# Attention scores and values as 64x64 products on TensorE, with the upper values split in two

## Chip, cores and metric

The kernel runs on one core of one Trainium2 chip. The metric is the device time of one execution in microseconds (us); the time before is the median of three executions. An additional execution was taken by the hardware profiler, and all lines of a profile below come from that one execution.

A core has five engines that run side by side and wait for one another through semaphores: TensorE (PE in the profile; PEld is its loading of weights), VectorE (DVE), ScalarE (ACT), GpSimd (POOL), and SyncE (SP), which here only issues DMAs. Each engine works through its own instructions in the order of the program. A matmul takes a stationary operand (weights) and streams the columns of a moving operand past it, into a bank of PSUM. The array of 128x128 cells can be used in tiles of 128x64, 64x128 or 64x64 cells; products at different places of the array run at the same time.

## What is computed

64 sequences of 128 tokens and 512 features go through one layer of multi-query attention: 16 query heads of 64 features share one key head and one value head, with a bias per head, a learned null key and value in front, a causal mask and a key mask. The result is projected, normalized and added to the input.

```python
xn = layernorm(x, g_in)                                # x: [64, 128, 512]
q = (xn @ Wq).reshape(b, n, H, DH).transpose(0, 2, 1, 3) * scale   # H = 16, DH = 64
k, v = split(xn @ Wkv)                                 # one head of 64 each
k, v = concat(null_k, k), concat(null_v, v)
sim = einsum('bhid,bjd->bhij', q, k) + concat(null_bias, attn_bias)
sim = where(causal, sim, neg); sim = where(mask, sim, neg)
out = einsum('bhij,bjd->bhid', softmax(sim), v)
out = out.transpose(0, 2, 1, 3).reshape(b, n, H * DH) @ Wo
return x + layernorm(out, g_out)
```

Everything is float32.

## The kernel before

The order of all instructions is written out by hand: `step(n)` (L838) is called for n from -6 to 62, and each call issues pieces of several stages for different sequences: normalizing (n+10, n+12), queries of a group of four sequences (`qg`), keys and values (n+5, n+6), scores (n+2), softmax (n+1), values (n), output projection (n-1 and earlier). There is no scheduler, so the order in the source is the order on each engine.

**Scores.** The 16 heads fall into two groups u of 8, and within a group a head is told by the row half r (which half of the array's rows its 64 features lie in) and by f (0 to 3). Partitions 0 to 63 of the score tile `S[b]` hold group u=0, partitions 64 to 127 group u=1, for 64 queries each. `scores(b, 0)` (L476) makes the lower scores: queries 0 to 63, which see keys 0 to 63 alone, as 16 products of 64x64 weights and 64 columns. `scores(b, 1)` makes the upper scores: queries 64 to 127 with all 128 keys. Before the change it does so as 8 products whose weights are 64 rows by 128 columns (both groups side by side). The row half r also chooses the PSUM bank: `pv[:, r]`. There is a single score buffer (pool `ps_s`, one buffer, tag "s"), so the upper (second) scores wait until DVE's `scores_add(b, 0)` (L509) has taken the lower (first) ones out. DVE then forms row maxima (`scores_max`), ACT the exponentials (L525), POOL multiplies with the reciprocal sums (L546).

**Turning the weights round.** `blocks_T(b)` (L569) turns S[b] on DVE in blocks of 32x32 into the tile `sb` (one buffer), and `blocks_move(b)` (L578) issues 14 DMAs on the SP queue that carry the blocks to the partitions where they belong, into `aTb` (one buffer except at the end). `aTb[keys, slot, head, query]` has six slots of 32 queries: slots 0 and 1 for the lower queries (group u=0 on partitions 0 to 63, u=1 on 64 to 127), slots 2 and 3 for the upper queries of u=0, slots 4 and 5 for those of u=1, with 128 keys each. The DMAs take eight semaphores in turn, so each also waits until the DMA eight places before it has landed.

**Values.** `values(b)` (L631) uses two PSUM tiles of pool `ps_w` (tag "w", two buffers), `po_b_0` and `po_b_1`, one for each group u, a bank each. `half` 0 holds the lower queries: 4 products with 64 key rows, the lower rows (`lo`) into bank 0, the upper rows (`hi`, with values moved up in `nv`) into bank 1. `half` 1 holds the upper queries: 4 products with all 128 key rows and 64 output partitions. Each product has 256 columns. ACT then moves both banks to `oT[b]` (L655). The two `ps_w` buffers are next used by `pk` (keys and values of a later sequence, L1017) and by a query product (`pw`).

**Around them in a step.** The queries and the output projection are made with seven products in place of eight (`product` L405, `out_product` L702), the sums and differences for which POOL forms: `token_sum` (L391), `out_sums` (L692). Pairs of sequences are projected together: a step with even n has `third` (a pair is normalized and added to the input on DVE: `pair_norm`, `pair_residual` L765), a step with odd n has `second` (`out_sums` and most of a pair's products). So steps come in kinds:

| n mod 4 | what differs near the end of the step |
|---|---|
| 0, 2 (even) | `pair_residual(p4 + 1)` runs on DVE (L767, L768) ahead of `blocks_T(n + 1)` |
| 1 | just before, `tokens_in` has issued four DMAs `xT<-xd` (L294) on SP, then `nulls_move` two; `mask_neg` runs on DVE once per group |
| 3 | nothing of these |

The stretch in question is the end of `step` (L981 to L1011):

```python
        if ok(n + 2):
            scores(n + 2, 0)
            scores_add(n + 2, 0)
        ...
        if third:
            pair_residual(p4 + 1)
        if soft and n + 1 < B - 2:
            blocks_T(n + 1)
        if ok(n + 2):
            scores_max(n + 2, 0)
        ...
        if ok(n):
            values(n)
        ...
        if n + 1 in sbs:
            blocks_move(n + 1)
        if ok(n + 2):
            scores(n + 2, 1)
```

`blocks_T(n + 1)` overwrites `sb`, so it waits for the DMAs of `blocks_move(n)`; `blocks_move(n + 1)` overwrites `aTb`, so it waits for the value products of n. POOL's `bias_add(n + 3)` reuses the score tile and waits for `blocks_T(n + 1)`. After the stretch PE goes on with a query product `pa` (k = 6), `pk`, `pa` (k = 7), and, over the next step's start, products into `pa` and `pc`; `pc` is freed by DVE's L442 (`q_out` into `qT`), which needs ACT's copy `ku` (L432) too.

Of the kernel before, what the change touches and what calls it, by code (L numbers as in the profile page):

```python
# [17 lines left out]
def kernel(  # L18
# [11 lines left out]
    g_out: bass.AP,  # L30
    out: bass.AP,
):

# [442 lines left out]
    def scores(b, hf):  # L476
        g, t = divmod(b, GB)
        nk = N if hf == 1 else NL
        ps = ps_s.tile([P, 2, NF, N], FP, tag="s", name=f"ps_{b}_{hf}")
        pv = ps.rearrange("p r f j -> p r (f j)")[:, :, 0 : NF * nk].rearrange(  # L480
            "p r (f j) -> p r f j", f=NF
        )
        for f in range(NF):
            if hf == 1:
                for r in range(2):
                    rows = slice(r * DH, (r + 1) * DH)
                    nc.tensor.matmul(  # L487
                        pv[:, r, f, :],
                        qT[g][rows, f, t, 1].rearrange("p u i -> p (u i)"),
                        kT[b][rows, :],  # L490
                        start=True,
                        stop=True,
                    )
            else:
                for r in range(2):
                    rows = slice(r * DH, (r + 1) * DH)
                    for u in range(2):
                        nc.tensor.matmul(  # L498
                            pv[u * DH : (u + 1) * DH, r, f, :],
                            qT[g][rows, f, t, 0, u],  # L500
                            kT[b][rows, 0:NL],
                            start=True,
                            stop=True,
                        )
        pss[b, hf] = pv

    pss = {}
# [120 lines left out]
            pt.rearrange("p e (s q) -> p e s q", q=Q),  # L628
        )

    def values(b):  # L631
        g, t = divmod(b, GB)
        oT[b] = bp.tile([P, NC, N], FP, tag="oT", name=f"oT_{b}")
        po = [
            ps_w.tile([P, 2, 2, NF, Q], FP, tag="w", name=f"po_{b}_{u}")
            for u in range(2)
        ]
        lo, hi = slice(0, DH), slice(DH, P)
        parts = [
            (0, 0, lo, vs[g][lo, t, 0:DH], slice(0, 2)),  # L640
            (1, 0, hi, nv[g][hi, t, 0:DH], slice(0, 2)),
            (0, 1, slice(0, P), vs[g][:, t, 0:DH], slice(2, 4)),
            (1, 1, slice(0, P), vs[g][:, t, 0:DH], slice(4, 6)),
        ]
        for u, half, rows, vals, slots in parts:
            for r in range(2):
                nc.tensor.matmul(  # L647
                    po[u][r * DH : (r + 1) * DH, half],
                    vals,
                    aT_of(b)[rows, slots, r * NF : (r + 1) * NF],  # L650
                    start=True,
                    stop=True,
                )
# [184 lines left out]
    def step(n):  # L838
# [145 lines left out]
            if ok(n + 1) and fill:  # L984
                rinv(n + 1, 1)
                scale(n + 1, 1)
        if third:
            pair_residual(p4 + 1)
        if soft and n + 1 < B - 2:
# [2 lines left out]
            scores_max(n + 2, 0)  # L992
        if n == 0:
            blocks_T(1)
        if n == B - 2:
            attn_T_pe(n)
        if ok(n):
            values(n)
        elif fast:
            product(qg, f, 6, ps_q, "a", start=False)  # L1000
            keep("a", "u2")
        if n + 1 in sbs:
            blocks_move(n + 1)
# [96 lines left out]

    load_res(B - 1)
    attn_T_pe(B - 1)
    values(B - 1)
    out_mm(B - 2)
    out_stats(B - 2)
    residual(B - 2)
# [41 lines left out]
```

## Time and profile before

| | us |
|---|---|
| time, median of 3 (lowest, highest) | 1186.27 (1185.86, 1194.16) |
| the profiled execution | 1192.74 |
| its span | 1190.3 |
| busy in the span: PE / PEld | 1124.7 / 880.3 |
| busy: DVE / ACT / POOL | 793.4 / 686.1 / 745.5 |
| L487, second scores, 1024 records of 64x128 | 79.5 |
| L498, first scores, 2048 records of 64x64 | 44.5 |
| L647, values: 128x64 records / 64x64 records | 74.7 / 81.7 |
| L572, `blocks_T`, 62 of 1.77 | 109.7 |
| PE idle for `po`, waiting for DMA `aTb<-sb`, 10 times | 13.9 |

A float32 matmul of the program stands in the trace as two records, each with its own weight load. "Busy" of PE counts overlapping records once; a record's length includes the time until its end left the array, so neighbouring records overlap, and the distance from start to start tells the pace better than the length. The granted TensorE clock was 0.98 of full speed over the span.

A timeline line reads: start in us from the span's start, length, engine, line of the source, operation, output<-inputs, tile of the array (rows*columns), shape, count, and in brackets the engine's idle time just before with what ended it. The chain of waits is followed back from the last instruction: each piece is what held the end up at that time.

### The profile page before, as it was taken

To read this page: it belongs to the slowest core of one execution; us is meant where nothing else is said; L and a number is where in the kernel's file an instruction comes from. 1 tells how busy PE (TensorE), PEld (TensorE's weight loads), DVE (VectorE), ACT (ScalarE), POOL (GpSimd) and SP (SyncE) were. 2 spreads that over 40 slices of the span, in tenths; PEclk is the share of its full clock that TensorE was granted. 3 is DMA by queue.
4 is the path that set the end of the run, shared out by engine and by line. 5 is a ranking of instruction groups with operands and counts; after the bars stand their busy time and mean duration, and the time that the engine had idled before them with its cause. 6 is when DMAs were issued, how large, how long until landed. Compare 5 with 4: busy or idle time off the path is not lost.

```text
span 1190.3 us, 24481 instructions
## 1 busy us (share of the span) xinstructions
PE 1124.7 (94%) x8284; PEld 880.3 (74%) x8284; DVE 793.4 (67%) x1680; ACT 686.1 (58%) x2712; POOL 745.5 (63%) x588
## 2 busy tenths in 40 slices
PE   6878999999999999999999999999999999999787
PEld 4455787887878788887778788787878877886433
DVE  6554577677767877676667677677766766666442
ACT  3344665665667656665665656566656656665351
POOL 5445876567676756667565665857566675856431
PEclk9997999999999999999999999999999999999889
DMA  6314235443533445353443535344453534322221
GB/s 189 113 63 93 78 99 128 123 117 97 154 102 118 114 125 129 112 136 97 133 91 124 121 89 156 98 132 99 126 127 119 123 87 138 81 59 78 78 75 45
DMA packets 107852, 129.91 MB, mean 109 GB/s; under 512 B 29264, under 2 KB 72528, under 8 KB 105936
## 3 DMA queue, kind: packets, MB, share of 16 engines
q1 hardware_dynamic: 106480, 126.96, 39.0%
q8 instruction: 67, 1.10, 0.4%
q10 hardware_dynamic: 1248, 1.38, 0.3%
q14 instruction: 57, 0.47, 0.1%
HBM read 54.86 MB, written 31.46 MB: 73 GB/s over the span
## 4 chain that ended last, share of the span: by engine, by line
PE 64%; DMA 11%; SPq 10%; DVE 6%; ACT 4%; POOL 2%; issue 2%; ACTq 0%; DVEq 0%; POOLq 0%
PE pa L421 13%; PE pyX L717 12%; SPq L598 8%; PE po L647 7%; PE pyY L717 6%; DMA xT<-xd 6%; PE pc L421 6%; PE ps L487 5%; PE pk L307 4%; PE py L667 3%; PE pw L421 3%; ACT s L525 3%; PE pyw L717 2%; DMA aTb<-sb 2%; PE ps L498 2%
## 5 line engine op out<-in xcount | busy, mean ns | idle before, releaser
L525 ACT ACTIVATE s<-s,nmax 128x65 f32<-128x65 f32 (+1 forms) x1024 | 372.9, 370 | 7.0 <-DVE nmax L516 6.6
L458 POOL TENSOR_TENSOR s<-biasp,mneg 128x1536 f32<-128x1536 f32 x64 | 220.9, 3453 | 121.8 <-DVE sb L572 116.8
L546 POOL TENSOR_TENSOR s<-s,rinv 128x512 f32<-128x512 f32 (+1 forms) x128 | 189.2, 1479 | 112.4 <-DVE nmro L759 80.8
L525 ACT ACTIVATION_READ_ACCUMULATOR s<-s,nmax 128x1 f32 x1024 | 196.6, 192 | 0.0
L655 ACT ACTIVATE oT<-po,nv 128x512 f32<-128x512 f32 x128 | 81.4, 682 | 163.2 <-PE po L647 162.8
L717 PE MATMUL pyX<-wT,oT 128*128 128x256 f32 x696 | 165.6, 381 | 1.2 <-POOL oT L699 0.7
L432 ACT COPY ku<-pa 128x256 f32<-128x256 f32 x120 | 44.8, 373 | 179.8 <-PE pa L421 179.8
L717 PEld LDWEIGHTS pyX<-wT,oT 128*128 128x128 f32 x696 | 132.5, 191 | 20.4 <-POOL oT L699 1.1
L511 DVE TENSOR_TENSOR s<-ps,s 128x512 f32<-128x512 f32 (+1 forms) x128 | 121.8, 951 | 20.6 <-PE ps L498 14.8
L421 PE MATMUL pa<-xS,wq 128*128 128x256 f32 x480 | 123.6, 380 | 2.4 <-ACT ku L432 1.4
L516 DVE TENSOR_REDUCE nmax<-s 128x8 f32<-128x520 f32 (+1 forms) x128 | 120.5, 941 | 6.0 <-POOL s L467 3.7
L647 PE MATMUL po<-aTb,vs 128*64 128x256 f32 (+1 forms) x768 | 112.1, 404 | 3.0 <-DVE aTb L626 1.7
L572 DVE STREAM_TRANSPOSE sb<-s 128x1536 f32<-128x1536 f32 x62 | 109.7, 1770 | 3.7 <-POOL s L546 3.6
L421 PEld LDWEIGHTS pa<-xS,wq 128*128 128x128 f32 x480 | 86.8, 190 | 13.0 <-ACT ku L432 2.4
L487 PEld LDWEIGHTS ps<-kT,qT 64*128 64x128 f32 x1024 | 66.7, 199 | 32.1 <-issue 20.4
L487 PE MATMUL ps<-kT,qT 64*128 64x128 f32 x1024 | 79.5, 298 | 5.4 <-DVE s L511 5.3
L442 DVE TENSOR_TENSOR qT<-pw,kp 128x256 f32<-128x256 f32 x60 | 25.4, 423 | 77.0 <-ACT kp L432 76.9
L647 PEld LDWEIGHTS po<-aTb,vs 128*64 128x64 f32 (+1 forms) x768 | 45.6, 141 | 40.7 <-issue 27.6
L245 POOL TENSOR_TENSOR rstd<-rstd,nhalf 128x1 f32<-128x1 f32 x64 | 35.9, 561 | 56.1 <-DVE rstd L244 56.1
L421 PE MATMUL pc<-xS,wS 128*128 128x256 f32 x240 | 63.3, 386 | 8.0 <-POOL xS L403 7.2
L307 PE MATMUL pk<-wkv,xT 128*128 128x144 f32 x488 | 69.9, 286 | 0.0
L421 PE MATMUL pa<-xS,wS 128*128 128x256 f32 x240 | 68.8, 409 | 0.0
(122 smaller groups left out, 2167.7 us busy)
## 6 DMA issues: line engine op xcount, KB each, us to landing
aTb<-sb SPq DMA_DIRECT2D x369, 64.0 KB
x<-in_x_dram SPq DMA_DIRECT2D x64, 256.0 KB
res<-in_x_dram SPq DMA_DIRECT2D x64, 256.0 KB
out_dram<-y SPq DMA_DIRECT2D x64, 256.0 KB
aTb<-sb SPq DMA_DIRECT2D x492, 32.0 KB
xd<-xb SPq DMA_DIRECT2D x14, 1024.0 KB
xT<-xd SPq DMA_DIRECT2D x56, 256.0 KB
wo<-in_L_cond_Wo_dram SPq DMA_DIRECT2D x1, 2048.0 KB
```

The lines of the kernel that those rows point to most:

```text
L307: nc.tensor.matmul(pkv, xT[g][:, t, kc, :], wkv[:, kc, :], start=(kc == 0), stop=(kc == KC - 1),)
L421: nc.tensor.matmul(prod[tag], w[:, kc, f * P : (f + 1) * P], t[:, :, kc, :], start=(start and kc == 0), stop=(kc == HK - 1), skip_group_ch ...
L458: nc.gpsimd.tensor_tensor(S[b][:, :, 1 : ROW - 1], biasp, mneg[g][:, t].unsqueeze(1).broadcast_to([P, R8, NL + N]), ALU.add,)
L487: nc.tensor.matmul(pv[:, r, f, :], qT[g][rows, f, t, 1].rearrange("p u i -> p (u i)"), kT[b][rows, :], start=True, stop=True,)
L511: nc.vector.tensor_tensor(sv, pss.pop((b, hf)), sv, ALU.add)
L516: nc.vector.tensor_reduce(nmax[b][:, hf], S[b][:, :, WITH_NULL[hf]], AX.X, ALU.max, negate=True)
L525: nc.scalar.activation(row, row, AF.Exp, bias=nmax[b][:, hf, k : k + 1], accum_out=rsum[b][:, hf, k : k + 1],)
L546: nc.gpsimd.tensor_tensor(sv, sv, rinvs.pop((b, hf)).unsqueeze(2).broadcast_to([P, R8, sv.shape[2]]), ALU.mult,)
L572: nc.vector.transpose(sb.rearrange("p j e q -> p e j q"), S[b][:, :, 1 : ROW - 1].rearrange("p e (j k) -> p e j k", k=Q),)
L598: queue.dma_start(out=aT_of(b)[dst, is_].rearrange("p s e q -> p s (e q)"), in_=sb[src, js].rearrange("p s e q -> p s (e q)"),)
L647: nc.tensor.matmul(po[u][r * DH : (r + 1) * DH, half], vals, aT_of(b)[rows, slots, r * NF : (r + 1) * NF], start=True, stop=True,)
L717: nc.tensor.matmul(prod[key], h[:, c, :], w[:, c, :], start=(start and c == 0), stop=(c == HC - 1), skip_group_check=not start,)
```

## The change

Three things are done.

1. `scores(b, 1)` is made like `scores(b, 0)`: 16 products of 64x64 weights (the two head groups u, each to its own 64 output partitions) and 128 columns, in place of 8 of 64x128.
2. The upper queries' values (`half` 1) are made of products with 64 key rows: 8 in place of 4. In a step that also has scores (`split`; n from 0 to 61), four of them stand in `values` before the second scores: lower key rows into bank 0, upper key rows into bank 1. The other four stand in a new function `values_end` after the second scores, and add to what is there: lower rows into bank 1, upper rows into bank 0. So a bank is fed by one half of the array's rows at a time.
3. Between the two parts stands a copy on DVE, `done`, of one column of bank 1. It reads what the first part wrote, and the second part overwrites what it read, so the second part of the products waits for it.

`values(n, split)` moves up in `step`, ahead of `pair_residual` and `blocks_T`; on PE that changes nothing before it, on DVE it puts `done` behind `scores_add(n + 2, 0)` and ahead of `pair_residual(p4 + 1)` and `blocks_T(n + 1)`. `values_end` and `blocks_move(n + 1)` now follow the second scores, and so do ACT's two moves to `oT`. `attn_T_pe` of step 62 moves up with the values. The order of the instructions on ACT, POOL and SP is the same as before; PE has 8 matmuls more per sequence for the scores and 4 more for the values of each step with `split`, DVE 62 copies more.

```diff
         for f in range(NF):
-            if hf == 1:
-                for r in range(2):
-                    rows = slice(r * DH, (r + 1) * DH)
+            for r in range(2):
+                rows = slice(r * DH, (r + 1) * DH)
+                for u in range(2):
                     nc.tensor.matmul(
-                        pv[:, r, f, :],
-                        qT[g][rows, f, t, 1].rearrange("p u i -> p (u i)"),
-                        kT[b][rows, :],
+                        pv[u * DH : (u + 1) * DH, r, f, :],
+                        qT[g][rows, f, t, hf, u],
+                        kT[b][rows, 0:nk],
                         start=True,
                         stop=True,
                     )
...
+    def value_mm(b, u, half, keys, vals, slots, start=True):
+        for r in range(2):
+            nc.tensor.matmul(
+                pos[b][u][r * DH : (r + 1) * DH, half],
+                vals[keys, b % GB, 0:DH],
+                aT_of(b)[keys, slots, r * NF : (r + 1) * NF],
+                start=start,
+                stop=True,
+                skip_group_check=not start,
+            )
...
+    def values(b, split):
...
+        value_mm(b, 0, 0, lo, vs[g], slice(0, 2))
+        value_mm(b, 1, 0, hi, nv[g], slice(0, 2))
+        if split:
+            value_mm(b, 0, 1, lo, vs[g], slice(2, 4))
+            value_mm(b, 1, 1, hi, vs[g], slice(4, 6))
...
+            done = small.tile([P, 1], FP, tag="done", name=f"done_{b}")
+            nc.vector.tensor_copy(done, pos[b][1][:, 1, 0, 0, 0:1])
+        else:
+            value_mm(b, 0, 1, slice(0, P), vs[g], slice(2, 4))
+            value_mm(b, 1, 1, slice(0, P), vs[g], slice(4, 6))
+
+    def values_end(b, split):
+        g = b // GB
+        if split:
+            value_mm(b, 1, 1, lo, vs[g], slice(4, 6), start=False)
+            value_mm(b, 0, 1, hi, vs[g], slice(2, 4), start=False)
+        po = pos.pop(b)
         for u in range(2):
             nc.scalar.activation(
...
+        if n == B - 2:
+            attn_T_pe(n)
+        split = ok(n + 2)
+        if ok(n):
+            values(n, split)
         if third:
             pair_residual(p4 + 1)
...
-        if n == B - 2:
-            attn_T_pe(n)
-        if ok(n):
-            values(n)
-        elif fast:
+        if not ok(n) and fast:
             product(qg, f, 6, ps_q, "a", start=False)
             keep("a", "u2")
-        if n + 1 in sbs:
-            blocks_move(n + 1)
         if ok(n + 2):
             scores(n + 2, 1)
             scores_add(n + 2, 1)
             scores_max(n + 2, 1)
+        if ok(n):
+            values_end(n, split)
+        if n + 1 in sbs:
+            blocks_move(n + 1)
```

More of the change, by code (lines that the diff above doesn't have):

```diff
@@ L493, in scores @@
                     )
[L494 to L504, printed above, removed]
         pss[b, hf] = pv
@@ L629, in attn_T_pe @@
         )
-    def values(b):
-        g, t = divmod(b, GB)
+    pos = {}
+    def value_mm(b, u, half, keys, vals, slots, start=True):
[8 more added lines that the diff above has]
+            )
+    lo, hi = slice(0, DH), slice(DH, P)
+    def values(b, split):
+        g = b // GB
         oT[b] = bp.tile([P, NC, N], FP, tag="oT", name=f"oT_{b}")
-        po = [
+        pos[b] = [
             ps_w.tile([P, 2, 2, NF, Q], FP, tag="w", name=f"po_{b}_{u}")
@@ L637, in values @@
         ]
[L638 to L653, printed above, removed]
+        value_mm(b, 0, 0, lo, vs[g], slice(0, 2))
[9 more added lines that the diff above has]
+    def values_end(b, split):
+        g = b // GB
+        if split:
+            value_mm(b, 1, 1, lo, vs[g], slice(4, 6), start=False)
+            value_mm(b, 0, 1, hi, vs[g], slice(2, 4), start=False)
+        po = pos.pop(b)
         for u in range(2):
@@ L1102 @@
     attn_T_pe(B - 1)
-    values(B - 1)
+    values(B - 1, False)
+    values_end(B - 1, False)
     out_mm(B - 2)
```

## The prediction, made before the changed kernel ran

> **What bounds the kernel now.** I read the page's busy shares and chain first, then the PE timeline of one step, then DVE and SP beside it, then the chain of waits in a stretch where PE stood idle. PE is busy 94% of the span, so the easy reading is "less PE time, less time". The page's chain is more careful:
>
> ```profile
> PE 64%; DMA 11%; SPq 10%; DVE 6%; ACT 4%; POOL 2%; issue 2%; ACTq 0%; DVEq 0%; POOLq 0%
> ```
>
> A third of the chain is not PE. The PE timeline of step 32 (an even one) from its first scores on:
>
> ```profile
> 645.48 0.69 PE L498 MATMUL ps<-kT,qT 64*64 64x64 f32 x32
> ...
> 646.69 1.08 PE L647 MATMUL po<-aTb,vs 128*64 128x256 f32 x8
> 647.71 1.16 PE L487 MATMUL ps<-kT,qT 64*128 64x128 f32 x16
> 648.80 1.13 PE L421 MATMUL pa<-xS,wS 128*128 128x256 f32 x4
> ...
> 653.51 1.13 PE L421 MATMUL pc<-xT,wS 128*128 128x256 f32 x4
> ```
>
> [...]The block from first scores to `pa` is 3.32 us; in odd steps it is 3.17. DVE in the same stretch:
>
> ```profile
> 646.24 0.69 DVE L511 TENSOR_TENSOR s<-ps,s 128x512 f32<-128x512 f32 x1
> 647.04 0.70 DVE L767 TENSOR_TENSOR yn<-yn,gob 128x512 f32<-128x512 f32 x1
> 647.78 0.69 DVE L768 TENSOR_TENSOR y<-yn,res 128x512 f32<-128x512 f32 x1
> 648.38 1.77 DVE L572 STREAM_TRANSPOSE sb<-s 128x1536 f32<-128x1536 f32 x1
> ...
> 653.04 0.41 DVE L442 TENSOR_TENSOR qT<-pc,ku 128x256 f32<-128x256 f32 x1
> ```
>
> See the end of the last row: 653.45. PE's `pc` product, which needs that buffer free, starts at 653.51. DVE runs without a gap from the transpose (`sb`) to `qT`, so after an even step PE is paced by the start of that transpose: `pc` starts 5.13 us after it. This distance from `qT`'s end to `pc` is 0.05 in most even steps and 0.05 to 0.7 in the rest; in odd steps it is 1.5.
>
> The second hold is the SP queue, steps 36 to 38 and 40 to 42:
>
> ```profile
> 717.96 1.77 DVE sb L572
> ...
> 733.16 9.52 DMA xT<-xd
> 742.70 2.06 DMA aTb<-sb
> ```
> ```profile
> 788.26 9.03 SPq L598 DMA_DIRECT2D aTb<-sb  x14
> ...
> 799.66 1.99 SPq L294 DMA_DIRECT2D xT<-xd  x4
> ...
> 804.46 13.40 SPq L598 DMA_DIRECT2D aTb<-sb  x14
> ```
>
> The first fence is the chain of waits, the second SP's timeline. In steps n divisible by 4 the transpose starts SP's 14 issues; behind them, back to back, stand two stores, two loads and the four `xT` loads, which take about 10 us to land; the next 14 issues wait for their landing in turn (13.40 us in place of 9.03), and `values` of step n+2 comes late. Against 2.23 us from first to second scores in an undelayed even step, 11 of the 12 steps 6, 10, ... 50 are 0.3 to 3.0 late, 13.7 in all. So the time between `sb` of a step divisible by 4 and `values` two steps on is set by DVE, SP and DMA, and PE time saved in it only lengthens PE's wait.
>
> **The change part by part.**
>
> *PE, columns streamed.* Second scores: 8 products of 64x128 weights, two at a time, become 16 of 64x64, four at a time. Upper values: 4 products, two at a time, become 8, four at a time. Either way each place of the array streams as much: 1.16-us row and 1.08-us row against 0.86 us of pure streaming (the distance between starts of neighbouring four-record product groups: four records of 256 columns one after another). No gain there.
>
> *PE, changes of tile.* First scores take 0.52 to the next start, the lower values 0.54 (0.43 streaming, 0.11 more), upper values 1.02 (0.86 + 0.16), second scores 1.09 (0.86 + 0.23). The first two excesses and some 0.06 of the last (its first weight load) go; the last drain, before the 128x128 `pa`, stays. Gross 0.33 us.
>
> *PE, what is late next.* Second scores wait for DVE's first add, as before (one buffer `ps`). That add ends 1.46 (odd steps 1.46 to 1.53) after the block's start; the four-at-a-time values before it end at 0.52 + 0.86 = 1.38, so PE waits to about 1.52 (0.06 from add to PE, as where this wait shows already: add ends 2.70, scores start 2.76). New block: 1.52 + 0.07 load + 0.86 + 0.43 + 0.17 drain = 3.05; with the add at 1.53, 3.12. Odd steps gain 0.13 (n = 1 mod 4) and 0.05 (3 mod 4); even ones 0.25, and 0.33 where the values are late and the add long done.
>
> *PE, instruction rate.* 512 + 248 more matmuls, two records each. Here a rule speaks against the change: the Trainium skill, "TensorE: Matmul & The Clock Gate", section "Wait — 56ns, not 53.3ns?", gives start-to-start never below about 25 ns, and about 62 ns where the sequencer decodes each matmul itself. By 62, the new 56 records of scores and values take 3.5 us in place of 2.15: +1.3 a step, +80 us in all. The row: 32 records of 64x64 scores in 0.52 us, 16 ns each with their loads. That is under both figures, and the new records stream longer than these; the row decides, cost 0.
>
> *DVE, the added copy `done`.* 62 copies of 128x1; the nearest row is a 128x1 operation at 0.15 us, so 0.16. Its length matters little; its place does. It stands behind the first add and ahead of `pair_residual` and the transpose, and waits for the eighth value product. Even steps: values start at 0.52, second pair 0.11 later (it does today), end 1.49; DVE follows PE by 0.24 (first scores over at 0.52, add at 0.76), so `done` runs 1.73 to 1.88. Today `yn` starts at 1.56. Everything behind moves by 0.32: `yn`, `y`, transpose, `qT`. Odd steps: transpose from 1.37–1.44 to about 1.75, +0.33, but DVE has 0.6 idle before `qT` there and 1.5 behind it: cost 0.
> Bounds for the shift: 0.1 if matmul completion reaches DVE at once; 0.6 if wait and copy each cost double. I take 0.32.
>
> *Even steps, n divisible by 4:* PE's `pc` moves with the transpose, +0.32, instead of PE's −0.25. SP's chain starts 0.32 later, and `values` of n+2 land 0.32 later. That covers steps n and n+1; what PE saves in n+1 is waited away.
> *Even steps, n = 2 mod 4 (late):* today `yn` runs inside PE's wait. With `done` ahead of it, it can't: transpose at landing + 0.86 + 0.24 + 0.16 + 1.3, about 2.55 after landing. Read against today's transposes this is 0.3 to 0.7 later (1.6 in step 30, none in step 26). Less the 0.05 to 0.7 that `qT` has in hand: about +0.35 a step.
>
> *ACT:* both evictions (L655) wait for the last products, 1.0 to 1.3 us later; they end near 4.4, and the next ACT copy `ku` starts at 4.3 to 4.5 today: at most 0.2, and its PE user comes 0.5 later. `pk` needs the first eviction's buffer: out at 3.8, wanted at 4.1. Cover 0.3 us; without it each step pays. POOL's `out_sums` starts about 0.9 later in even steps; 0.78 and 0.48 idle follow on POOL (step 36's), and its product comes 5.5 us after `oT`. Cost 0.
> *SP:* no issue changes place. `blocks_move` now also waits for the second value part (over by 2.9 to 3.1); the transpose ends at 3.5 or later. Cost 0. `attn_T_pe` moves past nothing that runs in step 62. Cost 0.
> *Odd steps with a late first add* (5, 29, 53; add to 2.5–2.7): the second value part now follows the scores there, +0.43; 5 and 29 lie in the waited-away stretch: +0.4.
>
> **Sum.** Twelve late cycles × (0.32 + 0.35 − 0.05) = +7.4; some ten steps outside them, half even at +0.3, half odd at −0.1: +1.0; late add +0.4. Total +8.8 us. The profiled execution took 1192.74 (span 1190.3), 6.5 over the median of the runs shown, 1186.27. I take the difference over: 1195, 0.7% more. A measurement of this kernel can tell about 1% (12 us) from no change: below 1174.4 is faster, above 1198.1 slower.
>
> **The rivals.**
> *The copy is hidden (0.22).* DVE reaches `done` when the values are over. Then the even steps keep DVE's pace and odd ones gain: 12 × −0.2 and −1 elsewhere, 1183. For it: DVE is 67% busy. Against: the add ends 0.03 before the values do even on PE's side, and `yn` starts at once.
> *The handshake costs more (0.2), slower.* Place: PE's completion to DVE's copy to the transpose, in even steps alone. At a shift of 0.6 the cycle pays 0.6 + 0.65 − 0.05, 14.4 in twelve, 2 to 3 elsewhere: 1203. It decides from 0.45: 12 × 0.9 + 1.9 passes 12 us. For it: three tight links; against: each is measured at 0.05 to 0.24.
> *The loads come out (0.08), slower.* If eight 64-column loads at each place of the second scores cost 0.06 each, and the values half that: +0.5 to 0.7 a step, about +25, 1211. It needs the second scores over 1.1 us. Against: 64x64 first scores hide theirs.
> *PE decides after all (0.07).* Gross 0.2 to 0.33 in all 62 steps, 1170 to 1176. Against: `pc` at 0.05 behind `qT`, and the late values.
>
> **The numbers.** The main case (0.43) is 1195 with 6 either way: 0.3 of it above 1198.1. With the rivals: slower 0.38, within 1% 0.55, faster 0.07. The range 1182 to 1208 takes in the hidden copy's value and most of the dear handshake.
>
> **What would show it.** Right: second scores as 64x64, 32 records near 0.9; block near 3.05; in even steps divisible by 4 the transpose 0.3 later after the first scores and `pc` still 0.05 behind `qT`. Wrong: transpose not moved; `pc` with slack; second scores over 1.1; PE waiting for `po` evictions before `pk`.

## The result, and the profile after

| | before | after |
|---|---|---|
| median of 14 runs each (lowest, highest), us | 1186.57 (1180.03, 1194.16) | 1189.74 (1183.71, 1194.40) |
| ratio after / before, 95% interval | | 1.0024 [1.0005, 1.0043] |
| the same kernel in a second comparison | | 1.0009 [0.9987, 1.0031] |
| the profiled execution / its span, us | 1192.74 / 1190.3 | 1189.17 / 1187.3 |

The change made the kernel 1 to 3 us slower: 0.24% in the first comparison and 0.09% in the second, whose interval takes in no change at all. Forecast were 8.8 us, 0.74%. The direction came out as forecast and the steps of the working can be read in the trace; the size was not right.

The profiled execution of after is 3.6 us *shorter* than that of before, while the medians stand the other way round. Single executions of one kernel here lie up to 14 us apart (1180.03 to 1194.16 for before), so a sum over one execution each can't be read off; what can be read is the shape of a step, which repeats to a few hundredths of a us where no transfer lands late.

The PE timeline of step 32 of the changed kernel (the step that is shown of before):

```profile
646.81 0.69 PE L488 MATMUL ps<-kT,qT 64*64 64x64 f32 x32
...
647.75 0.77 PE L625 MATMUL po<-aTb,vs 64*64 64x256 f32 x8
648.31 1.10 PE L488 MATMUL ps<-kT,qT 64*64 64x128 f32 x32
649.24 0.61 PE L625 MATMUL po<-aTb,vs 64*64 64x256 f32 x8
649.78 1.13 PE L422 MATMUL pa<-xS,wS 128*128 128x256 f32 x4
...
655.09 1.13 PE L422 MATMUL pc<-xT,wS 128*128 128x256 f32 x4 [0.50 <-DVE qT L443]
```

From first scores to `pa` it is 2.97 us in place of 3.32. The 32 records of the second scores take 0.93 to the next start. But at the end of the step PE now waits 0.50 for `qT`; the shorter block has become a wait. DVE in the same stretch says why:

```profile
647.57 0.69 DVE L501 TENSOR_TENSOR s<-ps,s 128x512 f32<-128x512 f32 x1
648.56 0.16 DVE L657 COPY done<-po 128x1 f32<-128x1 f32 x1 [0.30 <-PE po L625]
648.63 0.69 DVE L781 TENSOR_TENSOR yn<-yn,gob 128x512 f32<-128x512 f32 x1
649.36 0.69 DVE L782 TENSOR_TENSOR y<-yn,res 128x512 f32<-128x512 f32 x1
649.97 1.77 DVE L562 STREAM_TRANSPOSE sb<-s 128x1536 f32<-128x1536 f32 x1
...
654.62 0.41 DVE L443 TENSOR_TENSOR qT<-pc,ku 128x256 f32<-128x256 f32 x1
```

DVE stands 0.30 idle for the value products, copies, and everything behind the copy is later: the transpose starts 3.16 after the first scores, in place of 2.90. `qT` ends at 655.03, PE's `pc` starts 0.06 later. The list of what PE waits for (us in total, times, longest) has it in nearly every even step; in before the same wait was 2.2 us in 4 places:

```profile
PE pc L422 <- DVE qT L443: 15.7, 30, 0.7
```

The chain of the whole execution has moved from PE to DVE accordingly (PE had 64% of it, DVE 6%):

```profile
PE 50%; DVE 17%; DMA 12%; SPq 11%; POOL 3%; issue 3%; ACT 3%; ACTq 0%; DVEq 0%; POOLq 0%
```

To find the size, the execution is cut at the late value products (`po<-aTb,nv`) of steps 4 and 52. There are three profiled executions of each kernel (two of each are experiments below: before_again and before_pad for before, after_again and after_pad for after, the pads less what their fillers add behind the end):

| us | before, three executions: mean | after, three executions: mean | difference | predicted |
|---|---|---|---|---|
| start to step 4 | 165.8, 163.1, 165.4: 164.8 | 164.3, 165.2, 164.4: 164.6 | -0.1 | |
| step 4 to step 52 | 825.3, 826.3, 822.5: 824.7 | 828.5, 836.1, 829.6: 831.4 | +6.7 | +7.4 |
| step 52 to the end | 199.2, 196.7, 196.8: 197.6 | 194.6, 194.3, 194.0: 194.3 | -3.3 | with the start: +1.4 |

By these executions the twelve late cycles cost nearly what was predicted. The row alone is no proof of it. Three more kernels below have the steps of before from 4 to 52 (tail_new, tail_warm and warm_61: 812.8, 830.7 and 829.9), and three those of the changed kernel (tail_old, tail_old_2 and last_old: 821.4, 821.6 and 825.7). Over six executions each the difference is +2.6, while the executions of one kind lie 15 to 18 us apart. The lengths of single steps, further down, carry the reading. The last steps, which were given +1.4 together with the first ones, gave 3.3 back.

### The profile page after: what moved, and what is told of

Its sections match the earlier page's. It is cut to its first block, busy times and chain, and to the rows that moved or that the text cites. A ratio compares the mean times of both kernels' runs of the same rounds, so it can differ in the third digit from the quotient of the medians.

```text
span 1187.3 us, 27533 instructions
## 1 busy us (share of the span) xinstructions
PE 1104.3 (93%) x9804; PEld 876.5 (74%) x9804; DVE 795.4 (67%) x1742; ACT 680.8 (57%) x2712; POOL 746.4 (63%) x588
## 4 chain that ended last, share of the span: by engine, by line
PE 50%; DVE 17%; DMA 12%; SPq 11%; POOL 3%; issue 3%; ACT 3%; ACTq 0%; DVEq 0%; POOLq 0%
PE pyX L731 11%; SPq L588 8%; PE pa L422 8%; PE pc L422 6%; PE pyY L731 6%; PE po L625 5%; PE ps L488 5%; DMA nv<-vs 4%; DVE sb L562 4%; DMA xT<-xd 4%; DVE nmax L506 4%; PE py L681 3%; DVE s L501 3%; PE pyw L731 2%; PE pk L308 2%
## 5 line engine op out<-in xcount | busy, mean ns | idle before, releaser
L488 PEld LDWEIGHTS ps<-kT,qT 64*64 64x64 f32 x4096 | 100.0, 135 | 48.3 <-DVE s L501 25.5
L488 PE MATMUL ps<-kT,qT 64*64 64x64 f32 (+1 forms) x4096 | 123.4, 253 | 7.9 <-DVE done L657 5.1
L625 PE MATMUL po<-aTb,vs 64*64 64x256 f32 (+1 forms) x1264 | 127.9, 385 | 3.0 <-DVE aTb L616 1.7
L422 PE MATMUL pc<-xT,wS 128*128 128x256 f32 x240 | 64.6, 392 | 15.0 <-DVE qT L443 15.0
L625 PEld LDWEIGHTS po<-aTb,vs 64*64 64x64 f32 (+1 forms) x1264 | 61.1, 136 | 10.0 <-issue 2.1
```

The costliest lines, as they stand in the source:

```text
L422: nc.tensor.matmul(prod[tag], w[:, kc, f * P : (f + 1) * P], t[:, :, kc, :], start=(start and kc == 0), stop=(kc == HK - 1), skip_group_ch ...
L488: nc.tensor.matmul(pv[u * DH : (u + 1) * DH, r, f, :], qT[g][rows, f, t, hf, u], kT[b][rows, 0:nk], start=True, stop=True,)
L625: nc.tensor.matmul(pos[b][u][r * DH : (r + 1) * DH, half], vals[keys, b % GB, 0:DH], aT_of(b)[keys, slots, r * NF : (r + 1) * NF], start=s ...
```

## The experiments

### The copy on DVE

**done_act**: the copy on ScalarE's queue, where nothing is behind it for long.

```diff
-            nc.vector.tensor_copy(done, pos[b][1][:, 1, 0, 0, 0:1])
+            nc.scalar.copy(done, pos[b][1][:, 1, 0, 0, 0:1])
```

> The copy between the two value parts on ScalarE in place of VectorE; all products as in the change. Theory (the copy holds VectorE up in even steps): the transpose of an even step goes back from 3.16 to about 2.9 us after the first scores, the wait of the pc product for qT (15.7 us in 30 waits) falls under 3 us, and the drains saved show at last: 0.2 to 0.3 us per cycle of four steps less than before the change, 1182 to 1184 us, ratio to before 0.996 to 0.998. Rival (the 64x64 products themselves cost, by loads or instructions): as the change, ratio 1.002. Rival (landing of the xT loads alone sets the pace, the copy is harmless): ratio between 1.000 and 1.002, transpose back but late values later by as much.

Measured: 0.9964 [0.9942, 0.9986], 1185.58 us; the changed kernel in the same comparison 1190.34. DVE's timeline in step 32 (first scores at 645.0):

```profile
645.73 0.69 DVE L501 TENSOR_TENSOR s<-ps,s 128x512 f32<-128x512 f32 x1
646.52 0.70 DVE L781 TENSOR_TENSOR yn<-yn,gob 128x512 f32<-128x512 f32 x1
647.25 0.69 DVE L782 TENSOR_TENSOR y<-yn,res 128x512 f32<-128x512 f32 x1
647.86 1.77 DVE L562 STREAM_TRANSPOSE sb<-s 128x1536 f32<-128x1536 f32 x1
```

The transpose is back at 2.90. The wait for `qT` went to 7.7 us in 21 places, not under 3 as expected: that part was a miss, the step lengths in steps divisible by 4 (17.72, as before) were not. So one copy of 128x1, 0.16 us long, costs the changed kernel 5 us by where it stands.

**done_wide**: the copy takes 256 columns into a tile as wide, and is longer by that.

```diff
-            done = small.tile([P, 1], FP, tag="done", name=f"done_{b}")
-            nc.vector.tensor_copy(done, pos[b][1][:, 1, 0, 0, 0:1])
+            done = small.tile([P, 2 * NF * Q], FP, tag="done", name=f"done_{b}", bufs=1)
+            nc.vector.tensor_copy(done, pos[b][1][:, 1].rearrange("p i f q -> p (i f q)"))
```

> As the change, but the copy on VectorE takes all 256 columns of the upper values of bank 1 in place of one: about 0.42 us in place of 0.16. Theory: the transpose of even steps another 0.26 us later (3.4 after the first scores); the step with n divisible by 4 grows by 0.26 to 18.2, and the cycle of four by 0.3 to 0.5, so 4 to 7 us more than the change: 1194 to 1197 us, ratio to before 1.006 to 1.009. Rival (landing of the xT loads alone sets the pace): as the change, 1.002 to 1.003.

Measured: 1.0108 [1.0078, 1.0139] in six executions, above the 1.006 to 1.009 expected. Transpose at 3.43 (0.27 later again), steps divisible by 4 at 18.25. The time follows the length of the copy, as it does for something on the path.

**whole_done**: the products of before, with the copy behind the last value product and ahead of `pair_residual`. The edit in short:

```diff
+        if ok(n):
+            values(n)     # ends with tensor_copy(done, po[1][:, 1, 0, 0, 0:1])
         if third:
             pair_residual(p4 + 1)
...
         if ok(n):
-            values(n)
+            values_end(n) # ACT's two moves to oT
```

> The kernel before, scores and values with its own products and tiles, values in one part; only the copy on VectorE is added, behind the first add and ahead of pair_residual, waiting for the last value product. Nothing on TensorE waits for it. Theory: the values are over 2.1 to 2.2 us after the first scores, so the copy runs at 2.4 to 2.55 and the transpose of even steps starts at 3.8, 0.9 later; steps divisible by 4 grow by 0.85 to 18.6, the cycle of four by 1.0 to 1.7 us: 12 to 20 us more, 1199 to 1207, ratio 1.010 to 1.017. Rival (products cost, not the copy): ratio 1.000. Rival (landing alone): ratio under 1.004.

Measured: 1.0210 [1.0168, 1.0252] in six executions, more than expected. Transpose at 3.76, steps divisible by 4 at 18.57. No new product is in it, and it is the slowest of all: the wait and the copy cost by themselves, without the 64x64 products. (The copy starts 2.35 after the first scores here, in place of 1.75 in the changed kernel, because it waits for the last value product.)

**after_again**: the changed kernel once more.

> The changed kernel once more, for its time beside the others on one chip and a second trace. Both theories: ratio 1.000 to 1.004, about 1189.5 us; the wait of pc for qT 14 to 17 us again, and the transpose of even steps again at 3.16 us. What the late values (steps 6, 10, ... 50) add is expected to differ from the first trace (8.0 us) by some us either way, since the landings differ from execution to execution.

Measured: 1.0009 [0.9987, 1.0031].

### One part of the change alone

**scores_only** and **scores_2** (the same kernel twice): before with `scores(b, 1)` as in the first hunk of the change, nothing else.

> The kernel before with the upper scores alone as 64x64 products: values whole, no copy. If 64x64 weight loads come out, the second scores are over 1.1 us and each step longer, ratio 1.01 and more. By my theory second scores take 0.93, odd blocks go from 3.17 to about 3.05 to 3.1, the transpose in steps divisible by 4 stays at 2.90, pc stays 0.05 behind qT there, so nothing is gained in steps 4 to 52 (825 us, give or take the landings' 3). For the last stretch: at half clock 64x64 scores took 1.98 and 64x128 ones 2.08, so the scores alone leave it near 199 (198 to 200), if the values' place is what shortens it. Ratio 0.9995 (0.998 to 1.001); 0.996 if the scores make the gain at the end.

> The same kernel as scores_only. If its 0.9943 is its own, the same here (0.992 to 0.9965); odd blocks 3.11 in place of 3.17, transpose at 2.90, second scores 0.93, last stretch (step 52's late value products to the end) 192.6 against 199.2. If it was chance, 0.998 to 1.001, as its steps let expect: nothing in steps 4 to 52, 2 us at the end.

Measured: 0.9943 [0.9922, 0.9964] and 0.9953 [0.9930, 0.9975]. Its PE timeline in a step divisible by 4:

```profile
641.43 1.08 PE L636 MATMUL po<-aTb,vs 128*64 128x256 f32 x8
642.44 1.10 PE L487 MATMUL ps<-kT,qT 64*64 64x128 f32 x32
643.48 0.70 PE L421 MATMUL pa<-xS,wS 128*128 128x256 f32 x2
```

Second scores take 1.04 to the next start in place of 1.09, where 0.93 was expected: the gain is small, but the loads don't come out. The transpose stays at 2.90 and the odd block goes to 3.11, near what was expected; that the time falls by 6 us was not. The steps' own lengths show 0.13 us a cycle of it (by medians, a late step from its value products on 16.87 in place of 16.94, n = 3 mod 4 at 15.62 in place of 15.68, steps divisible by 4 unchanged at 17.72), under 2 us in twelve. In its two executions the stretch from step 4 to 52 was 819.7 and 816.3, 5 and 8 us under the mean of before's three, and the stretch behind step 52 was 192.6 and 196.4, 5 and 1 us under. So most of the gain does not lie in the steps' own lengths, and where it comes from is open.

**values_only**: the other part alone, the upper scores as before.

```diff
                 rows = slice(r * DH, (r + 1) * DH)
+                if hf == 1:
+                    nc.tensor.matmul(
+                        pv[:, r, f, :],
+                        qT[g][rows, f, t, 1].rearrange("p u i -> p (u i)"),
+                        kT[b][rows, :],
...
+                    continue
                 for u in range(2):
```

> The changed kernel with the upper scores as before (8 products of 64x128): values split, copy on VectorE. If the values' split with its copy is what costs and the scores what gains, as scores_only (0.994 and 0.995) says, then this lies above the changed kernel: by the steps' terms 1.004 (1.002 to 1.006), by adding the runs (changed 1.002 less scores_only 0.995) 1.007. Transpose in steps divisible by 4 at 3.16, pc close behind qT. Rival: the scores are worth nothing in the steps and scores_only's gain is landings; then 1.001 to 1.002, as the changed kernel.

Measured: 1.0054 [1.0032, 1.0075], between the two sums. Transpose at 3.16. `pc` waits for `qT` only 3.2 us in 4 places, since with the upper scores of before the block stays at 3.33. The two parts, 0.995 and 1.0054, come together near the 1.001 to 1.002 of the changed kernel: one gains half a per cent, the other spends about as much.

### The last steps

The first explanation of the 3.3 us was that the new products are shorter where PE's clock is low. The next three runs tried it, and it did not hold.

**tail_old** and **tail_old_2** (the same kernel twice): the changed kernel, with the products of before from step 56 on. **tail_new**: the reverse, before with the new products from step 56 on.

```diff
+    def quad(n):
+        return n < 56          # tail_new: n >= 56
...
-        split = ok(n + 2)
+        split = ok(n + 2) and quad(n)
```

(and `scores(b, 1)` takes its form from `quad(b - 2)`.)

> The changed kernel, with the products of before (upper scores 64x128, values whole, no copy) in steps 56 and later alone. Theory: the changed kernel's last steps are about 5 us shorter because of the new products there, so here the stretch from the late value products of step 52 to the end goes back from 194.6 to 199 us (198 to 200), while the late cycles of steps 4 to 52 stay as in the changed kernel (transpose at 3.16 in steps divisible by 4). Time: the changed kernel's plus 4.6, ratio to before 1.006 (1.004 to 1.009). Rival: the gain at the end comes from how the steps before enter it (stores and loads further ahead); then the stretch stays at 194.6 and the ratio at 1.002.

> The same kernel as tail_old. If its 0.9961 is the kernel's own, the same here (0.994 to 0.998), and then the products of before in the last steps are worth about 5 us against the changed kernel although one execution showed the last stretch 1 us longer. If it was chance of that loading, 1.000 to 1.003.

> The kernel before, with the new products and the copy in steps 56 and later alone. Theory: the last stretch (step 52's late value products to the end) falls from 199.2 to 194.5 us, steps 4 to 52 stay as before (transpose at 2.90 in steps divisible by 4, block 3.17 in odd steps). Ratio to before 0.996 (0.994 to 0.998). Rival (the gain comes in from earlier steps): stretch 199, ratio 1.000.

Measured: tail_old 0.9961 [0.9940, 0.9981] and 0.9969 [0.9950, 0.9989], the stretch behind step 52 at 195.5 and 194.8; tail_new 0.9975 [0.9953, 0.9996], the stretch at 194.4. tail_new came out as expected (though its steps 4 to 52, which are before's, fell too, to 812.8), tail_old did not: with the products of before in the last steps the end is only some 1 us longer than the changed kernel's 194.3, not 5, so the products as such are not the reason. And tail_old is 5 to 6 us faster than the changed kernel, although its steps up to 55 are the same: this the steps don't explain. What goes along with it is SP's wait for the reads of `x`, behind which the 14 issues stand. In the lists of SP's waits (engine and line, what was waited for, us, times, longest), the changed kernel:

```profile
SPq L588 <- DMA x<-in_x_dram: 14.7, 8, 4.9
```

and tail_old:

```profile
SPq L600 <- DMA x<-in_x_dram: 7.4, 5, 3.8
```

(5.4 in tail_old_2, 5.5 in tail_new; 22.2 and 17.8 in the other two executions of the changed kernel, 21.6 to 26.4 in those of before, 29.2 and 32.0 in warm_61 and tail_warm.) Among kernels with the same loop, the stretch from step 4 to 52 is longer where this wait is longer. Pairs with nearly the same wait also show the loops apart: at 5.4 and 5.5 us the changed kernel's loop took 821.6 (tail_old_2) and that of before 812.8 (tail_new); at 22.2 and 21.6 it was 836.1 (after_again) and 826.3 (before_again). So at equal waits the changed loop is some 9 us longer, near the forecast 7.4, and the mean over all executions hides it because its waits were shorter, 13 us in place of 23. That is what twelve executions have in common, not an experiment: why these reads land earlier in one kernel than in another with the same steps, and whether the change itself shortens the wait, is open.

**before_pad** and **after_pad**: short fillers on PE behind the last product, to see if a build as such moves the time.

```diff
     out_stats(B - 1)
     store(B - 1)
+    pad = ps_s.tile([P, Q], FP, tag="s", name="pad")
+    for _ in range(144):        # after_pad: 72
+        nc.tensor.matmul(
+            pad[0:DH], ident[0:DH, 0:DH], ident[0:DH, 0:Q], start=True, stop=True
+        )
```

> The kernel before, with 144 short filler products on PE behind its last product, where PE has nothing left to do while the last rows are normalized and stored; they fill some 4 us and their result is not used. Nothing in the steps changes, so no theory of the products gives it a gain or a loss: 1.000 (0.998 to 1.002). Rival: a build as such moves the landings of transfers (tail_old differs from the changed kernel in its last six steps alone, and its steps 4 to 52 took 821 us against 828 and 836); then this one may lie anywhere from 0.994 to 1.006 too.

> The changed kernel with 72 such fillers behind its last product. Without an effect of the build: as the changed kernel, 1.001 to 1.002 (0.999 to 1.004), step 61's late value products to the end 42.0 us. With such an effect: outside that, and the difference then lies in the landings between the transpose of steps divisible by 4 and the late value products two steps on (32.9 and 33.4 us on the mean in the two executions of the changed kernel, 32.3 in tail_old's).

Measured: 1.0173 [1.0133, 1.0213] and 1.0075 [1.0049, 1.0101]. The fillers were mis-sized: all at one place of the array, the 288 records of before_pad take 26.9 us, not 4, and set the end. From step 63's value products to the end it is 44.1 and 29.0 in place of 22.1; less these 22.0 and 6.9, the medians are 1185.7 (0.999 of before) and 1190.3 (1.003). So these two builds did not move the time.

**last_old**: the changed kernel with the products of before in step 61 alone (`quad(n)` is `n != 61`). **before_again**: before once more.

> The changed kernel with the products of before in step 61 alone. By the last steps: step 61's late value products to the end goes from 42.0 to between 43.1 and 46.1, ratio 1.004 (1.002 to 1.006). If what made tail_old fast is not in steps 56 to 60: 0.9965 (0.994 to 0.998), with short waits of SP for the reads of x (5 to 8 us in tail_old's two executions, 15 to 22 in the changed kernel's three).

> The kernel before once more, for a second look at its steps: time 1.000; steps 4 to 52 take 822 to 826, the stretch from step 52's late value products to the end 195 to 199 (199.2 in the first look), of it step 61's late value products to the end 43 to 46; SP's waits for the reads of x 20 us and more (26.4 in the first look).

Measured: last_old 0.9993 [0.9962, 1.0024], between both expectations; before_again 0.9987 [0.9959, 1.0016]. Here the traces say more than the times. PE in step 61 of before, in before_again:

```profile
1136.97 0.60 PE L647 MATMUL po<-aTb,vs 64*64 64x256 f32 x4
1142.53 1.12 PE L647 MATMUL po<-aTb,nv 64*64 64x256 f32 x4 [4.96 <-DVE y L779]
1143.58 1.97 PE L647 MATMUL po<-aTb,vs 128*64 128x256 f32 x8
1145.48 1.89 PE L487 MATMUL ps<-kT,qT 64*128 64x128 f32 x16
1147.31 3.27 PE L667 MATMUL py<-wo,oT 128*128 128x512 f32 x7
```

of the changed kernel:

```profile
1143.20 0.60 PE L625 MATMUL po<-aTb,vs 64*64 64x256 f32 x4
1145.31 0.43 PE L625 MATMUL po<-aTb,nv 64*64 64x256 f32 x2 [1.50 <-DVE y L793]
...
1148.48 1.98 PE L681 MATMUL py<-wo,oT 128*128 128x512 f32 x4 [0.79 <-ACT oT L669]
```

and of last_old:

```profile
1139.07 0.60 PE L637 MATMUL po<-aTb,vs 64*64 64x256 f32 x4
1141.14 0.65 PE L637 MATMUL po<-aTb,nv 64*64 64x256 f32 x4 [1.47 <-DVE y L805]
1141.72 1.08 PE L637 MATMUL po<-aTb,vs 128*64 128x256 f32 x8
1142.73 1.16 PE L491 MATMUL ps<-kT,qT 64*128 64x128 f32 x16
1143.82 2.41 PE L693 MATMUL py<-wo,oT 128*128 128x512 f32 x5
```

The same products that take 1.97 and 1.89 in before take 1.08 and 1.16 in last_old. In before PE has stood idle for 4.96 us; in the other two for 1.5. The first profile of before, the one that the prediction was made from, has it too:

```profile
1144.24 1.12 PE L647 MATMUL po<-aTb,nv 64*64 64x256 f32 x4 [3.84 <-DVE y L779]
1145.29 1.97 PE L647 MATMUL po<-aTb,vs 128*64 128x256 f32 x8
```

The granted clock in before_again's stretch (window, us, PE busy and records, clock, DMA share, GB/s):

```profile
1140.00:1145.00 5.00, 2.47 (x12) 0.52 0.66 221
```

and in the same stretch of the changed kernel:

```profile
1140.00:1145.00 5.00, 3.81 (x43) 1.00 0.58 189
```

From the late value products of step 61 to `py` it is 4.78 us in before, 3.17 in after, 2.68 in last_old. So in step 61 it is the clock behind a long wait, not the products. The Trainium skill, "TensorE: Matmul & The Clock Gate", section "HAM oscillation — how this bites in real kernels", gives gaps above about 3.4 us as what lowers the clock; 4.96 did (and 3.84 in the first profile of before), 1.5 did not, but in before_again the second scores of step 59 also ran at half pace (2.08 us) after gaps of 1.71 and 0.64, and the products of step 26 did (upper values 1.97, clock 0.50 from 543 to 548 us) behind a wait of 1.92, so 3.4 is no safe line here.

**tail_warm** and **warm_61**: before with fillers on PE in these waits; tail_warm in steps 59 (8), 60 (12) and 61 (12), warm_61 in step 61 alone, with 17.

```diff
+    def keep_warm(k):
+        if not k:
+            return
+        pb = ps_q.tile([P, P], FP, tag="c", name="warm")
+        for _ in range(k):
+            nc.tensor.matmul(pb, ident, ident, start=True, stop=True)
...
+            if u == 0 and half == 0:
+                keep_warm({61: 17}.get(b, 0))
```

> The kernel before, with filler products of the identity on PE where it waits in the last steps: 8 ahead of the late value products in step 59, 12 ahead of the second scores in step 60, 12 ahead of the late value products in step 61; their result is not used. Clock theory: before's last steps are long because PE's granted clock falls to half after these waits; with fillers the clock stays near 1.00, the upper values and second scores of steps 59 to 61 take 1.1 each in place of 2.0, and the stretch from step 52 to the end falls from 199.2 to about 194 us (192 to 196.5); ratio 0.996 (0.993 to 0.998). Rival: the end waits for landings and normalization, and PE's pace there is covered; then products run at full pace, but the stretch stays within 1 us of 199 and the ratio at 1.000 (or a little above, where fillers stand in the way).

> The kernel before, with 17 filler products of the identity (some 3.7 us, their result is not used) on PE in step 61 alone, between the lower and the late value products, where PE waited 3.8 and 5.0 us in two looks. If the granted clock after that wait is what made the last steps of before long: less than 1.7 us of wait left, upper values 1.08 and second scores 1.16 in place of 1.97 and 2.08, from the late value products to the projection py 2.7 in place of 4.8 to 5.0, step 61's late value products to the end 41.5 (41.0 to 42.2) in place of 43.1 to 46.1, time 0.998 (0.996 to 1.000). Rival: the fillers themselves or landings decide; then py comes as late as before and the stretch stays at 43 or more, 1.000 to 1.002.

Measured: tail_warm 1.0018 [0.9988, 1.0049], not the gain expected in the time. The stretch from step 52 to the end was 195.3 in its trace, which is within the 192 to 196.5 expected, but steps 4 to 52 took 830.7 there. In step 59 the fillers did what they were meant to. PE in step 59 of before (first profile):

```profile
1106.76 1.12 PE L647 MATMUL po<-aTb,nv 64*64 64x256 f32 x4 [2.28 <-DMA aTb<-sb]
1107.81 1.97 PE L647 MATMUL po<-aTb,vs 128*64 128x256 f32 x8
1109.71 2.08 PE L487 MATMUL ps<-kT,qT 64*128 64x128 f32 x16
```

of the changed kernel, its second scores:

```profile
1112.15 1.10 PE L488 MATMUL ps<-kT,qT 64*64 64x128 f32 x32 [1.22 <-DVE s L501]
```

and of tail_warm:

```profile
1112.29 1.08 PE L654 MATMUL po<-aTb,vs 128*64 128x256 f32 x8
1114.03 1.16 PE L487 MATMUL ps<-kT,qT 64*128 64x128 f32 x16 [0.66 <-DVE s L511]
```

From the late value products of step 59 to `py` it is 7.63 to 7.90 in before's three profiles, 5.60 in the changed kernel's and 5.25 in tail_warm, and from step 57 to step 61 tail_warm takes 65.75 in place of 68.2. In step 60 the fillers gained nothing: its products ran at full pace, but the late value products of step 61 came 20.81 us after those of step 60, as late as in before (20.97 or 20.98): what PE wins in step 60 it waits for in step 61. There 3.54 us of wait were left, and the products behind it took 1.97 and 2.08 again. warm_61 closes this wait:

```profile
1142.69 4.06 PE L559 MATMUL warm<-ident 128*128 128x128 f32 x34
1147.08 0.65 PE L654 MATMUL po<-aTb,nv 64*64 64x256 f32 x4 [0.33 <-DVE y L788]
1147.66 1.08 PE L654 MATMUL po<-aTb,vs 128*64 128x256 f32 x8
1148.68 1.16 PE L487 MATMUL ps<-kT,qT 64*128 64x128 f32 x16
1149.77 7.13 PE L676 MATMUL py<-wo,oT 128*128 128x512 f32 x16
```

Full pace, 2.69 us to `py` in place of 4.2 to 5.0, and from there on the end comes 41.55 us after step 61's late value products, as expected (46.1, 43.6 and 43.1 in before's three). The time is 0.998 [0.9959, 1.0002]: the size expected, though the interval just reaches 1. In the trace, products that do nothing shorten the end by 2 us; this shows the mechanism for step 61.

**split_last**: the version that the runs point to, 64x64 upper scores everywhere, values whole up to step 55 and split from 56 on.

```diff
-        split = ok(n + 2)
+        split = ok(n + 2) and n >= 56
```

> 64x64 upper scores in all steps, values whole up to step 55, split with the copy from step 56 on. If the gains add: scores_only's 0.995 and 2 to 3 us at the end (step 61's late value products to the end 42.0 in place of 44 to 46), 0.9925 (0.991 to 0.9945). If the last steps' gain is taken back by waits ahead of them: 0.995 (0.9935 to 0.9965).

Measured: 0.9900 [0.9865, 0.9936], 1177.93 us in six executions: ahead of both kernels, and by more than either sum expected. Its steps divisible by 4 have the transpose at 2.90 and the length of before (17.72), its end is the changed kernel's (42.0 from step 61's late value products).

## Why the forecast had the sign and not the size

Lengths of steps below are medians over steps 4 to 51, the same in each of the three executions to 0.03 us.

- *Block near 3.05.* 2.97 measured, 3.04 in steps 3 mod 4. The second scores start 1.50 after the block's start, when the first add is over (1.52 predicted) and take 0.93 as 64x64. The row of 16 ns per record was the right one to go by; "the loads come out" (1211) is out, and so is "PE decides after all": the shorter block ends in a wait for `qT`.
- *Transpose 0.32 later in steps divisible by 4.* 0.26. `done` starts at 1.75 (1.73 predicted) and takes 0.16, but `yn` starts 0.07 after `done`'s start, not 0.16. The step got 0.26 longer (17.72 to 17.98). "The copy is hidden" and "the handshake costs more" both put this elsewhere and are out; done_act and done_wide move it both ways, and the time with it.
- *n = 2 mod 4: +0.35.* From the late value products on, the step takes 17.34 in place of 16.94: +0.40. The transpose stands 2.5 behind them (2.55 predicted), about 2.0 in before. In single late steps PE ran at half pace behind the wait, as in step 26 above; such steps and other late ones add 2.7, 6.3 and 0.3 us in before's three executions and 0, 1.8 and 0 in the changed kernel's, and the forecast had nothing of them.
- *n = 3 mod 4: -0.05.* 15.68 to 15.56: -0.12.
- *Odd steps' transpose near 1.75.* It came at 2.03 in most; harmless, as said, since nothing waits for it there. ACT's evictions cost nothing in these steps: PE waits for them 2.0 us in 3 places, all for `py`, of the last steps.
- *Twelve late cycles: +7.4.* From the steps' terms 12 x (0.26 + 0.40 - 0.12) = +6.5. The mechanism of this part held; the stretch itself gives +6.7 over three executions each and +2.6 over six, where executions of one loop lie 15 to 18 us apart.
- **The step that failed: "some ten steps outside them, half even at +0.3, half odd at -0.1: +1.0"**, with the +0.4 of the late add. It carried the loop's rates into the last steps. From step 52 to 57 they do hold (85.2 to 85.9, +0.7). But the late add of step 53 cost 0.1, and from step 57 to 61 the means go from 68.2 to 66.4, from step 61 to the end from 44.3 to 42.0. There PE stands in waits of 1 to 5 us, and what counts is how long they are, since the clock falls behind them. Rows of the last steps of before would have shown it, such as those of steps 59 and 61 above: PE idle 2.28 and 3.84, then the upper values at 1.97 us where the loop has 1.08. With -3.3 in place of +1.4 the same sum gives some +4, 1190. Of the 2.3 us behind step 61, 1.5 are its way to `py` (4.96, 4.78 and 4.18 in before, 3.17 in each of after's), and the clock as their cause is shown (warm_61, last_old); that PE waits less there because it comes out of step 60 later is what the two timelines suggest, and was not tried alone. The rest is, as far as is known, chance: in one of before's three profiles PE ran step 62's upper values at half pace too (1.97). Of the 1.8 us of steps 57 to 61, step 59 at half pace is seen in all of before's profiles and in none of after's, and tail_warm gets them back by fillers; how the 2 us won there pass on to step 61 was not followed.
- *Not in the sum at all:* the landings. Steps 4 to 52 took 821 to 836 us in six profiled executions of the changed kernel's loop (changed kernel, after_again, after_pad, last_old, tail_old twice) and 813 to 831 in six of before's. An uncertainty of some 6 us for a single execution, the standard deviation of either six, belongs in such a forecast, and a difference of 9 us between two kernels is not far above it.
- *The sign* is in part luck. Whole kernels with the changed loop came out at 0.996, 0.997 and 0.999 (tail_old twice, last_old) as well as at 1.001 and 1.002, and kernels with before's loop at 0.9975 to 1.002 (tail_new, warm_61, tail_warm). A difference of 0.1 to 0.2% between two kernels can't be put down to the steps alone.

## What to carry over

A one-column copy that a matmul has to wait for costs what stands behind it on its engine, not its own length: put it on the queue with the least behind it, and look at the engine that paces the step before splitting products to save PE time. A change of the loop is to be costed separately in the steps where the loop runs out, from rows of those steps: there PE waits, the clock falls, and a change of the waits can outweigh the change of the work. And a part of a change can be worth more than the whole: here the 64x64 scores alone gained what the split values spent.

## What was not expected of the hardware

- Behind waits of 1.9 to 5 us PE in many places ran the next products at half pace (clock 0.50 and 0.52 in two such windows), and 17 products without use in one wait made the end of the trace 2 us earlier.
- Two neighbouring instructions on DVE overlap: a 128x1 copy of 0.16 us put the next start off by 0.07 only.
- 64x64 records at four places in turn start every 29 ns with 128 columns; records of 32 columns, all at one place, took 93 ns each in before_pad and 82 in after_pad.
- One kernel's executions differ by 10 us and more, and the landing of reads that no step of the change touches (SP waits for `x` of 5 to 32 us in total) is the visible part of it.
